# A Mamba layer and six local-attention layers in one kernel: folded value weights, heads on partition quarters, softmax transposed by VectorE

## The chip, the cores and the metric

The kernel runs on one core of one Trainium2 chip. The metric is the time on the device in microseconds (us) of one execution; the median of several is compared. A core has five engines that each follow their own list of instructions in order: TensorE (PE; its weight loads are shown apart as PEld), VectorE (DVE), ScalarE (ACT), GpSimd (POOL) and SyncE (SP), which here issues every DMA. They meet through semaphores alone.

## What is computed

Input x is 4 sequences of 1024 tokens with 128 features. Everything is float32 but the mask.

```python
x = L0_attn_x                                   # (4, 1024, 128)
x = x + mamba_block(layernorm(x))               # two directions, states of 16, 256 channels
x = x + ffn_block(layernorm(x))                 # the six layers below

def ffn_block(x):
    for i in range(6):
        x = attn_layer(shift_tokens(x), Wqkv[i], q_scale[i], k_scale[i], Wo[i]) + x
        x = ffn_layer(shift_tokens(x), ln_g[i], ln_b[i], W1[i], b1[i], W2[i], b2[i]) + x
    return x

def attn_layer(x, Wqkv, qs, ksc, Wo):           # 16 heads of 64
    q, k, v = split_heads(x @ Wqkv)
    q, k = l2norm(q) * qs, l2norm(k) * ksc
    q = q * cos * scale + rotate_half(q) * sin * scale
    k = k * cos / scale + rotate_half(k) * sin / scale
    # windows of 32 queries; the keys are the window before and the window itself, 64 in all
    sim = where(mask, -big, 8.0 * q @ k.T)
    out = softmax(sim) @ v
    return join_heads(out) @ Wo

def ffn_layer(x, g, bln, W1, b1, W2, b2):
    a, gate = split((layernorm(x) * g + bln) @ W1 + b1)
    return a * gelu(gate) @ W2 + b2
```

`shift_tokens` takes half of the features from the token before. The value path of one head is linear in x: softmax times (x @ Wv_h), times Wo_h, summed over heads.

## The kernel before

The work has three stretches. In the first, class `Prepare` runs the Mamba projections, convolutions and gates of eight units (4 sequences, 2 directions) in the order of the table `FIRST_ORDER`, and spills them to DRAM. It also prepares layer data, one layer in each of six units: W1 scaled by the norm's gain, biases, and rotary tables multiplied by the q and k scales (`lf`, `fp`, `fv`, `fa`, `fs`, `lr`, `rm`, `rs`). Class `Beside` runs the Mamba state scan as 512 steps of 128x512: decay (ACT, line 699), input (DVE or POOL, 710 to 714), scan (DVE, 731), output (POOL, 744) and a sum over states on PE (line 766, which writes into partition quarters).

In the second stretch class `Layers` runs the six layers of a sequence that is through while the scan of the following ones goes on; in the third the layers run alone. `Layers` works on 96 tiles (4 sequences, 6 layers, 4 blocks of 256 tokens). For each tile some 130 small operations are named in a table, `ORDER` in the second stretch and `LAST_ORDER` in the third; the number behind the dash says how many tiles back the operation reaches, so about five tiles are under way at a time. The place in the table is the place in every engine's list. Words with x (`xd`, `xi`, `xr`, `xo` and so on) call the scan's steps, six of each a tile.

One tile's attention, with lines: `q` projects 128 tokens onto 512 columns of q or k in eight products (974). `sq` squares them on ACT (981); `rr` and `ro` multiply by the rotary tables on DVE (994); `n` sums the squares (1002); `nr` makes the reciprocal norm on ACT (1014 to 1016); `ra` adds rotated halves on POOL in eight operations (1007); `rs` applies the norm (1020). `t` transposes on PE (1057) and `qk` copies to SBUF (1067). `v` projects the values (1026), `va` copies them (1032) and `vs` issues a DMA that shifts them by 32 partitions (1042, 1043), so that a window's 64 keys stand together. `s` puts the mask into PSUM by a product (1078) and `s` and `z` add the 128 products of 32 queries and 64 keys (1096). `mx` takes the row maxima and `e` subtracts them on DVE (1106, 1112); `ex` takes the exponentials of 128x1024 in one go on ACT (1118); `sm` sums and inverts (1122, 1123), `ew` scales on POOL (1127). `te` transposes the probabilities on PE (1134), `at` copies (1140); `w` and `y` multiply them by the values (1159), `oe` copies (1170) and `pw` multiplies by Wo (1181).

In the feed-forward part `pd` centres the tokens by a product (1207), `fsq` squares, `pvar` averages (1221), `fl` makes the reciprocal deviation, `xnc` and `xn` normalize (1217, 1232). `pg` projects the gate, `ge` adds its bias (1247) and `gelu` follows in two pieces with a table load before and after (1253 to 1256); `pa`, `gm`, `py` and `xs` finish.

PSUM has eight banks; five rotate among all products of `Layers` (`one`), three belong to the scan. Weights of a layer have one buffer each; `weight` counts their uses and, after the last of a layer, queues the loads of the next layer for 30 or 60 table entries later (`later`).

Of the kernel before, what the change touches and what calls it, by code (L numbers as in the profile page):

```python
# [85 lines left out]
def make_masks(nc, pool, c):  # L86
    nc.vector.tensor_copy(c["ident16"], c["ident"])
    nc.vector.memset(c["mean"], 1.0 / D)
    nc.vector.tensor_tensor(c["center"], c["ident"], c["mean"], ALU.subtract)

    m32 = pool.tile([P, 8, 2 * W], F32, name="m32")
    nc.gpsimd.memset(m32, 0.0)
    for r in range(4):
        q = m32[r * W : (r + 1) * W]
        nc.gpsimd.affine_select(
            out=q, in_=q, pattern=[[0, 8], [1, 2 * W]], compare_op=ALU.is_ge,
            fill=NEG, base=0, channel_multiplier=-1,
        )
        nc.gpsimd.affine_select(
            out=q, in_=q, pattern=[[0, 8], [-1, 2 * W]], compare_op=ALU.is_ge,  # L100
            fill=NEG, base=W, channel_multiplier=1,
        )
    nc.vector.tensor_copy(c["mask"], m32)

    nc.vector.tensor_copy(c["mask0"], m32)
    nc.vector.memset(
        c["mask0"][0:W].rearrange("p (h x) j -> p h x j", x=2)[:, :, 0, 0:W], NEG
    )
# [23 lines left out]
class Prepare:  # L132
# [4 lines left out]
    def __init__(self, ctx, tc, c, eps, one, dram, x, lnwb, win, wconv, wx, wdt, rope, qks, tabs,  # L137
                 w1, lvec, w1f, lvf, x1_dram, beside, load):
# [4 lines left out]
        self.folds = w1, lvec, w1f, lvf  # L143
        self.rope = {}
# [204 lines left out]
    def xb(self, u, h):  # L349
        xdbl = u.tile(self.sp, "xdbl", 0, [NX, T], 2)  # L350
        self.nc.vector.tensor_copy(xdbl[:, h * TC : (h + 1) * TC], u.bank["wx", h])
# [50 lines left out]
    def lf(self, u):  # L402
        if u.l is not None:
            w1s = u.tile(self.sp, "w1s", 0, [P, 2 * FI], 2)
# [29 lines left out]

    def fs(self, u):
        if u.l is not None:
            self.nc.sync.dma_start(out=self.folds[2][u.l], in_=u.tiles["w1s", 0])
            self.nc.sync.dma_start(out=self.folds[3][u.l], in_=u.tiles["lv", 0])

# [86 lines left out]
class Beside:  # L526
# [165 lines left out]
    def decay(self):  # L692
        n = self.next("decay", self.limit)
# [28 lines left out]
    def scan(self):  # L722
        n = self.next("scan", self.limit)
# [11 lines left out]
    def output(self):  # L735
        n = self.next("output", self.limit)
# [144 lines left out]
class Layers:  # L881
# [3 lines left out]
    def __init__(  # L885
        self, ctx, tc, c, eps, ps, beside, wqkv, tabs, wo, w1f, w2, lvf, xsa, x1_dram, out
# [3 lines left out]
        self.dram = (wqkv, tabs, wo, w1f, w2, lvf)  # L890
# [12 lines left out]
        self.count = dict.fromkeys(USES, 0)  # L903
# [8 lines left out]
    def weight(self, name, t):  # L912

        w = self.weights[name]
        self.count[name] += 1
        if self.count[name] % (NSB * USES[name]) == 0 and self.tile_at(t, 1):
            for part in self.parts(name, (t.l + 1) % DEPTH):
                self.later(part, LATER if name in ("wos", "w2s") else LATE)
        return w
# [6 lines left out]
    def load(self, name, l):  # L926
        for part in self.parts(name, l):
            part()

    def parts(self, name, l):  # L930

        wqkv, _, wo, w1f, w2, lvf = self.dram
        tile_ = partial(self.wp.tile, dtype=F32, name=name)
        if name in ("w0", "w1", "w2"):
            a = int(name[1]) * H * DH
            w = tile_([P, H * DH])
            pairs = [
                (w[:, i : i + 256], wqkv[l, :, a + i : a + i + 256]) for i in range(0, H * DH, 256)
            ]
        elif name == "wos":  # L940
            w = tile_([P, NHP, D])
            of = wo[l].rearrange("(h p) m -> p h m", p=P)
            pairs = [(w[:, i : i + 2], of[:, i : i + 2]) for i in range(0, NHP, 2)]
# [11 lines left out]
        self.weights[name] = w  # L955
        return [partial(self.nc.sync.dma_start, out=to, in_=of) for to, of in pairs]
# [13 lines left out]
    def q(self, t, i, a, g):  # L970

        w = self.weight(f"w{a}", t)
        pq = t.bank["q", i, a, g] = self.one("pq")
        self.nc.tensor.matmul(  # L974
            pq, lhsT=self.tokens(t, i), rhs=w[:, g * 512 : (g + 1) * 512], start=True, stop=True
        )

    def sq(self, t, i, a, g):
        sq = t.tile(self.sp, "sq", (i, a), [P, H, DH], 2)
        pq = t.bank["q", i, a, g].rearrange("p (h e) -> p h e", e=DH)  # L980
        self.nc.scalar.activation(sq[:, g * 8 : g * 8 + 8], pq, AF.Square)  # L981

    def rr(self, t, i, a, g):

        self.rotary(t, i, a, g, t.tile(self.sp, "r", (i, a), [P, H, DH], 4), 0)

    def ro(self, t, i, a, g):

        self.rotary(t, i, a, g, t.tile(self.sp, "rot", (i, a), [P, H, DH], 2), 1)

    def rotary(self, t, i, a, g, out, x):
        pq = t.bank["q", i, a, g].rearrange("p (h e) -> p h e", e=DH)
        tab = bc(t.tab[:, i, 2 * a + x, :], 1, [P, 8, DH])
        self.nc.vector.tensor_tensor(out[:, g * 8 : g * 8 + 8], pq, tab, ALU.mult)  # L994
        t.rotary += 1
        if t.rotary == 16 and self.tile_at(t, 2):
            self.later(partial(self.table, self.tile_at(t, 2)))

    def n(self, t, i, a):

        n2 = t.tile(self.sp, "n2", i, [P, 2, H], 4)
        self.nc.vector.tensor_reduce(n2[:, a, :], t.tiles["sq", (i, a)], AX.X, ALU.add)  # L1002

    def ra(self, t, i, a, x):
        r, rot = t.tiles["r", (i, a)], t.tiles["rot", (i, a)]
        to, of = slice(x * W, x * W + W), slice(W - x * W, 2 * W - x * W)
        self.nc.gpsimd.tensor_tensor(r[:, :, to], r[:, :, to], rot[:, :, of], ALU.add)  # L1007
# [10 lines left out]
    def rs(self, t, i, a):  # L1018
        r, n2 = t.tiles["r", (i, a)], t.tiles["n2", i]
        self.nc.gpsimd.tensor_tensor(r, r, bc(n2[:, a, :], 2, [P, H, DH]), ALU.mult)  # L1020

    def v(self, t, i, g):

        w = self.weight("w2", t)
        pv = t.bank["v", i, g] = self.one("pv")
        self.nc.tensor.matmul(  # L1026
            pv, lhsT=self.tokens(t, i), rhs=w[:, g * 512 : (g + 1) * 512], start=True, stop=True
        )

    def va(self, t, i, g):  # L1030
        v = t.tile(self.sp, "v", i, [P, H * DH], 4)
        self.nc.scalar.copy(v[:, g * 512 : (g + 1) * 512], t.bank["v", i, g])

    def vs(self, t, i):

        nc, v = self.nc, t.tiles["v", i]
        vs = t.tile(self.sp, "vs", i, [P, H * DH], 4)
        if t.sb == 0 and i == 0:
            nc.gpsimd.memset(vs[0:W], 0.0)
        else:  # L1040
            before = t.tiles["v", 0] if i else self.tile_at(t, -1).tiles["v", 1]
            nc.sync.dma_start(out=vs[0:W], in_=before[P - W : P])
        nc.sync.dma_start(out=vs[W:P], in_=v[0 : P - W])
# [8 lines left out]
    def t(self, t, i, a, g):  # L1052

        rf = t.tiles["r", (i, a)].rearrange("p h e -> p (h e)")
# [16 lines left out]
    def s(self, t, g):  # L1071
# [10 lines left out]
        self.products(t, g, range(2))  # L1082

    def z(self, t, g):
        self.products(t, g, range(2, 4))

    def products(self, t, g, js):
        qT, kT = t.tiles["qT", 0], self.kT
        for j in js:
            for x in range(2):  # L1090
                for r in range(4):
                    at = P * (r // 2) + 64 * x + W * (r % 2)
                    for par in range(2):
                        rows = slice(64 * par, 64 * par + 64)
                        col = (j * 2 + x) * 64
                        self.nc.tensor.matmul(  # L1096
                            t.bank["s", g, par][r * W : (r + 1) * W, col : col + 64],
                            lhsT=qT[rows, g * 4 + j, at : at + W],
                            rhs=kT[rows, g * 4 + j, at : at + 2 * W],
                            start=False, stop=(j == 3 and x == 1),  # L1100
                        )

    def mx(self, t, g, par):
        mx = t.tile(self.sp, "mx", g, [P, 16], 2)
        sv = t.bank["s", g, par].rearrange("p (n j) -> p n j", j=2 * W)
        self.nc.vector.tensor_reduce(mx[:, par * 8 : par * 8 + 8], sv, AX.X, ALU.max)
# [22 lines left out]
    def te(self, t, g, par):  # L1129

        ef = t.tiles["e", g].rearrange("p (h x) j -> p h (x j)", x=2)
        pe = t.bank["te", g, par] = self.one("pe")
        for j in range(4):
            self.nc.tensor.transpose(  # L1134
                pe[:, j * P : (j + 1) * P], ef[:, par * 4 + j, :], self.c["ident"]
            )

    def at(self, t, g, par):
        at = t.tile(self.sp, "at", (g, par), [P, 4, P], 4)
        self.nc.scalar.copy(at, t.bank["te", g, par].rearrange("p (h t) -> p h t", t=P))  # L1140

    def w(self, t, g):

        for x in range(2):
            t.bank["w", g, x] = self.one("po")
        self.weighted(t, g, range(2))

    def y(self, t, g):
        self.weighted(t, g, range(2, 4))

    def weighted(self, t, g, js):
        for j in js:
            for r in range(4):
                v = t.tiles["v" if r % 2 else "vs", r // 2]
                for par in range(2):
                    col = (g * 8 + 2 * j + par) * DH
                    for x in range(2):
                        rows = slice(64 * x, 64 * x + 64)
# [425 lines left out]
```

## Time and profile before

| what | us |
|---|---|
| median of the runs shown (4049.41 to 4068.73) | 4055.16 |
| span of the profiled execution | 4070.2 |
| mean granted TensorE clock | 0.959 of full |

The profiled execution is one run on the chip, 15 us over that median. An engine's busy share is an average over stretches with different limits, so the text that follows reads it by stretch. In a row of a group or of the timeline stand the line, the engine, the operation, the tile written and read, shapes, and behind the x the number of instructions. A float32 product shows as two PE instructions, a transpose as one. In the granted clock, by slices of a fortieth of the span:

```profile
PEclk6788869999999999999999999999999999999999
DMA  5688855555545555555555555554221222122211
```

### The profile page before, as it was taken

How to read it: one execution, taken by the hardware profiler on the slowest of the kernel's cores; microseconds unless marked ns; L12 is line 12 of the kernel's file. 1: busy time of each engine (PE TensorE's matmuls, PEld its weight loads, DVE VectorE, ACT ScalarE, POOL GpSimd, SP SyncE). 2: the span in 40 equal slices, each digit the busy share in tenths (PEclk: the TensorE clock that was granted, in tenths of full speed). 3: DMA queues.
4: the chain of work that ended last, by engine and by line, in shares of the span. 5: the costliest groups of instructions: out<-in, count | busy, mean ns of one | idle time of the engine just before them, and what ended most of it. 6: DMA issues, size and time to landing. Idle time of an engine off the chain costs nothing.

```text
span 4070.2 us, 145466 instructions
## 1 busy us (share of the span) xinstructions
PE 3825.5 (94%) x62248; PEld 2447.0 (60%) x62248; DVE 3397.9 (83%) x5081; ACT 2975.5 (73%) x5581; POOL 3164.3 (78%) x2589
## 2 busy tenths in 40 slices
PE   5899859999999999999999999999999999999998
PEld 1333226666666666666666666666666666666665
DVE  3677769999899999999999999999777777777774
ACT  4577737887777787787777887877667777677775
POOL 2767669999889898998998998988666666566662
PEclk6788869999999999999999999999999999999999
DMA  5688855555545555555555555554221222122211
GB/s 156 190 268 267 250 178 149 148 161 154 149 133 159 145 154 153 161 151 148 154 145 142 156 156 158 153 151 118 58 65 54 64 58 74 52 63 57 66 50 40
DMA packets 319415, 540.05 MB, mean 133 GB/s; under 512 B 41795, under 2 KB 123467, under 8 KB 318771
## 3 DMA queue, kind: packets, MB, share of 16 engines
q1 hardware_dynamic: 318770, 530.75, 45.5%
q8 instruction: 492, 8.06, 0.9%
q14 instruction: 153, 1.25, 0.1%
HBM read 381.42 MB, written 51.67 MB: 106 GB/s over the span
## 4 chain that ended last, share of the span: by engine, by line
PE 70%; ACT 12%; DVE 7%; POOL 6%; issue 4%; DMA 1%; SPq 1%; DVEq 0%; ACTq 0%; POOLq 0%
PE pq L974 12%; PE po L1159 10%; PE pw L1181 8%; PE pv L1026 7%; PE pt L1057 6%; PE sim L1096 5%; PE pe L1134 4%; PE pm L290 3%; PE py L1278 3%; PE pa L1262 3%; PE pg L1238 2%; ACT sq L981 2%; PE acc L766 2%; DVE sh L731 1%; PE sim L1078 1%
## 5 line engine op out<-in xcount | busy, mean ns | idle before, releaser
L1007 POOL TENSOR_TENSOR r<-r,rot 128x512 f32<-128x512 f32 x768 | 964.1, 1274 | 83.2 <-DVE rot L994 71.1
L1020 POOL TENSOR_TENSOR r<-r,n 128x1024 f32<-128x1024 f32 x384 | 726.2, 1905 | 261.3 <-ACT n L1016 253.2
L974 PE MATMUL pq<-w,xsa 128*128 128x512 f32 x1536 | 799.0, 615 | 2.7 <-ACT at L1140 1.6
L744 POOL TENSOR_TENSOR sh<-sh,sc 128x512 f32<-128x512 f32 x512 | 649.9, 1274 | 96.9 <-DVE sh L731 66.7
L981 ACT ACTIVATE sq<-pq 128x512 f32<-128x512 f32 x768 | 448.2, 599 | 254.0 <-PE pq L974 125.4
L994 DVE TENSOR_TENSOR rot<-pq,tab 128x512 f32<-128x512 f32 x768 | 516.4, 683 | 133.9 <-ACT sq L981 111.0
L994 DVE TENSOR_TENSOR r<-pq,tab 128x512 f32<-128x512 f32 x768 | 518.1, 683 | 82.1 <-PE pq L974 40.3
L1127 POOL TENSOR_TENSOR e<-e,sm 128x1024 f32<-128x1024 f32 x192 | 365.5, 1904 | 243.6 <-DVE sm L1123 228.4
L1057 PEld LDWEIGHTS pt<-ident,r 128*128 128x128 f32 x3072 | 359.1, 142 | 242.5 <-issue 119.1
L1057 PE MATMUL pt<-ident,r 128*128 128x128 f32 x3072 | 443.4, 277 | 37.0 <-POOL r L1020 15.2
L1002 DVE TENSOR_REDUCE n<-sq 128x16 f32<-128x1024 f32 x384 | 456.6, 1210 | 0.0
L1159 PEld LDWEIGHTS po<-at,vs 64*64 64x64 f32 x12288 | 332.3, 135 | 198.3 <-issue 153.8
L1159 PE MATMUL po<-at,vs 64*64 64x32 f32 x12288 | 400.0, 223 | 21.5 <-issue 12.3
L1159 PE MATMUL po<-at,v 64*64 64x32 f32 x12288 | 391.6, 220 | 5.9 <-issue 5.8
L1026 PE MATMUL pv<-w,xsa 128*128 128x512 f32 x768 | 383.4, 601 | 0.2 <-ACT qT L1067 0.2
L1181 PE MATMUL pw<-o,wos 128*128 128x256 f32 x1536 | 377.9, 389 | 1.7 <-ACT o L1170 1.7
L731 DVE TENSOR_TENSOR_SCAN sh<-da,carry,sh 128x512 f32<-128x512 f32 x256 | 327.1, 1278 | 43.7 <-ACT da L699 41.2
L731 DVE TENSOR_TENSOR_SCAN sh<-da,sh 128x512 f32<-128x512 f32 x256 | 311.5, 1217 | 57.2 <-ACT da L699 50.6
L1096 PEld LDWEIGHTS sim<-kT,qT 64*32 64x32 f32 x24576 | 264.5, 106 | 141.8 <-issue 134.7
L1159 PEld LDWEIGHTS po<-at,v 64*64 64x64 f32 x12288 | 334.6, 136 | 9.0 <-issue 8.9
L699 ACT ACTIVATE da<-sdt,b_nega 128x512 f32<-128x512 f32 x378 | 260.5, 689 | 108.2 <-DVE sh L731 92.7
L974 PEld LDWEIGHTS pq<-w,xsa 128*128 128x128 f32 x1536 | 257.0, 191 | 125.8 <-issue 49.0
(160 smaller groups left out, 7598.5 us busy)
## 6 DMA issues: line engine op xcount, KB each, us to landing
sdt<-dts SPq DMA_DIRECT2D x756, 256.0 KB
vs<-v SPq DMA_DIRECT2D x192, 384.0 KB
fdt<-dts SPq DMA_DIRECT2D x204, 256.0 KB
w<-in_wqkv SPq DMA_DIRECT2D x288, 128.0 KB
tab<-tabs SPq DMA_DIRECT2D x96, 256.0 KB
vs<-v SPq DMA_DIRECT2D x168, 128.0 KB
wos<-in_wo SPq DMA_DIRECT2D x96, 128.0 KB
dts<-e SPq DMA_DIRECT2D x32, 256.0 KB
```

The costliest lines, as they stand in the source:

```text
L731: self.nc.vector.tensor_tensor_scan(h, self.da.pop(n), h, self.carry[:, at : at + 1] if t else 0.0, ALU.mult, ALU.add)
L744: self.nc.gpsimd.tensor_tensor(h, h, self.unit[k][2], ALU.mult)
L974: self.nc.tensor.matmul(pq, lhsT=self.tokens(t, i), rhs=w[:, g * 512 : (g + 1) * 512], start=True, stop=True)
L981: self.nc.scalar.activation(sq[:, g * 8 : g * 8 + 8], pq, AF.Square)
L994: self.nc.vector.tensor_tensor(out[:, g * 8 : g * 8 + 8], pq, tab, ALU.mult)
L1007: self.nc.gpsimd.tensor_tensor(r[:, :, to], r[:, :, to], rot[:, :, of], ALU.add)
L1020: self.nc.gpsimd.tensor_tensor(r, r, bc(n2[:, a, :], 2, [P, H, DH]), ALU.mult)
L1026: self.nc.tensor.matmul(pv, lhsT=self.tokens(t, i), rhs=w[:, g * 512 : (g + 1) * 512], start=True, stop=True)
L1057: self.nc.tensor.transpose(pt[:, j * P : (j + 1) * P], rf[:, (g * 4 + j) * P : (g * 4 + j + 1) * P], self.c["ident"],)
L1096: self.nc.tensor.matmul(t.bank["s", g, par][r * W : (r + 1) * W, col : col + 64], lhsT=qT[rows, g * 4 + j, at : at + W], rhs=kT[rows, g * ...
L1159: self.nc.tensor.matmul(t.bank["w", g, x][64 * par : 64 * par + 64, j * P + r * W : j * P + (r + 1) * W], lhsT=v[rows, col : col + DH], rh ...
L1181: self.nc.tensor.matmul(t.bank["pw"], lhsT=wos[:, g * 4 + h, :], rhs=t.tiles["o", g][:, h, :], start=(g == 0 and h == 0), stop=(g == 1 and ...
```

## The change

What it does, by part:

- *Values.* The value and output weights of each head are multiplied on chip during the preparation (`wl` loads, `wp` multiplies, `we` copies, `ws` stores; six layers, 16 heads, 128x128 each) and read back by `Layers` as `wvo`. `v` then takes 32 tokens at a time and four products of 512 columns, one for each partition quarter: quarter c has the heads of four columns of `wvo`. `va` copies eight windows a tile. The shifted copies (`vs`) and the output projection (`pw`) go.
- *Scores.* A partition quarter holds one head's 32 queries; a row of a bank has eight windows of 64 keys.
- *Softmax.* `mx` gives the negated maximum; `ea` takes the exponentials window by window from PSUM on ACT, 128x64 each, 32 a tile, with the maximum as bias, and writes out the row sums. `e`, `ex` and the sum in `sm` go; `rc` inverts.
- *Transposing.* `tp` transposes 32x32 blocks of 128x1024 on DVE, twice a tile; `te` and `at` go. `w` multiplies quarters (contraction over four heads and 32 keys at a time, 32 queries by 128 features), `oe` copies once and `ot` transposes the 256x128 result back on PE.
- *Rotary.* q and k columns are stored half by half (on the host), so `ra` is four operations of 128x1024.
- *Feed-forward.* W1 is also centred in the preparation (`fc`, `fe`), so that `xn` takes the uncentred tokens and `xnc` goes. `pg` and `pa` share banks by pairs; Gelu reads PSUM and adds the bias itself.
- *Loads.* Each layer's weights are loaded at a named place in the tables (`lw`, `lwv`, `l`, `ll`, `lt`); values and vectors have two buffers, the others one.
- *Tables.* `FIRST_ORDER`, `ORDER` and `LAST_ORDER` are new throughout; the scan's steps gain guards that skip a call that comes too early.

```diff
+    def wp(self, u, g, par):
+        if u.l is not None:
+            pm = u.bank["wp", g, par] = self.one("pm")
+            rows = slice(64 * par, 64 * par + 64)
+            for k in range(4):
+                self.nc.tensor.matmul(
+                    pm[:, k * D : (k + 1) * D], lhsT=u.tiles["wvl", 0][rows, g * 4 + k, :],
+                    rhs=u.tiles["wol", 0][rows, g * 4 + k, :], start=True, stop=True,
+                )
...
+    def fc(self, u, g):
+        if u.l is not None:
+            pm = u.bank["fc", g] = self.one("pm")[:, 0:FI]
+            self.nc.tensor.matmul(
+                pm, lhsT=self.c["center"], rhs=u.tiles["w1s", 0][:, g * FI : (g + 1) * FI],
+                start=True, stop=True,
+            )
...
-    def ra(self, t, i, a, x):
-        r, rot = t.tiles["r", (i, a)], t.tiles["rot", (i, a)]
-        to, of = slice(x * W, x * W + W), slice(W - x * W, 2 * W - x * W)
-        self.nc.gpsimd.tensor_tensor(r[:, :, to], r[:, :, to], rot[:, :, of], ALU.add)
+    def ra(self, t, i, a):
+        r = t.tiles["r", (i, a)].rearrange("p h x e -> p (h x e)")
+        rot = t.tiles["rot", (i, a)].rearrange("p h x e -> p (h x e)")
+        self.nc.gpsimd.tensor_tensor(r, r, rot, ALU.add)
...
+    def v(self, t, w):
+        wvo = self.weight("wvo", t)
+        pv = t.bank["v", w] = self.one("pv")
+        at = W + t.sb * SB + w * W
+        for c in range(4):
+            self.nc.tensor.matmul(
+                pv[c * W : (c + 1) * W], lhsT=self.xsa[t.b % 2][:, at : at + W], rhs=wvo[:, c],
+                start=True, stop=True,
+            )
...
+    def ea(self, t, g, par):
+        e = t.tile(self.sp, "e", g, [P, 16, 2 * W], 2)
+        sm = t.tile(self.sp, "sm", g, [P, 16], 2)
+        mx = t.tiles["mx", g]
+        sv = t.bank["s", g, par].rearrange("p (n j) -> p n j", j=2 * W)
+        for w in range(8):
+            n = par * 8 + w
+            self.nc.scalar.activation(
+                e[:, n], sv[:, w], AF.Exp, bias=mx[:, n : n + 1], accum_out=sm[:, n : n + 1]
+            )
...
+    def tp(self, t, g):
+        eT = t.tile(self.sp, "eT", g, [P, 2, 8, 2, W], 2)
+        self.nc.vector.transpose(
+            eT.rearrange("p a w x q -> p (a w x q)"),
+            t.tiles["e", g].rearrange("p n j -> p (n j)"),
+        )
+
+    def w(self, t, g, i):
...
+        for par in range(2):
+            for x in range(2):
+                for r in range(4):
...
+                    self.nc.tensor.matmul(
+                        t.bank["o"][r * W : (r + 1) * W, i * D : (i + 1) * D],
+                        lhsT=eT[:, par, 4 * i + r, x, :],
+                        rhs=of.tiles["vw", at % 8][:, 2 * g + par, :],
+                        start=first, stop=(t.weighted == 4 and par == 1 and x == 1),
+                    )
...
     def gelu(self, t):
-        nc.scalar.activation(ge[:, 0:2, :], ge[:, 0:2, :], AF.Gelu)
-        nc.scalar.activation(ge[: FM[2], 2, :], ge[: FM[2], 2, :], AF.Gelu)
+        for m in range(3):
+            k = FM[m]
+            nc.scalar.activation(
+                ge[:k, m, :], self.half(t, "pg", m), AF.Gelu, bias=lv[:k, 3 + m : 4 + m]
+            )
```

## The prediction

> **What bounds the kernel now.** I read the busy table first, then the chain that ended last, then busy time by stretches, to see whether one engine bounds every stage.
>
> ```profile
> PE 3825.5 (94%) x62248; PEld 2447.0 (60%) x62248; DVE 3397.9 (83%) x5081; ACT 2975.5 (73%) x5581; POOL 3164.3 (78%) x2589
> PE 70%; ACT 12%; DVE 7%; POOL 6%; issue 4%; DMA 1%; SPq 1%; DVEq 0%; ACTq 0%; POOLq 0%
> ...
> 800.00:2800.00 2000.00, 1941.36 (x34683) 1298.99 (x34682) 1878.56 (x2733) 1550.25 (x2956) 1822.59 (x1503) 0.99 0.54 151
> 3000.00:4000.00 1000.00, 990.19 (x18409) 687.76 (x18402) 764.86 (x1182) 732.03 (x1403) 639.59 (x455) 1.00 0.21 60
> ```
>
> The last two rows give, for a stretch of the span, busy us (and instructions) of PE, PEld, DVE, ACT and POOL, then the granted clock. PE is busy 97% in the first, where Mamba runs beside the layers, and 99% in the second, where the layers run alone. DVE (94%) and POOL (91%) are close behind in the first. ACT has the most room: 78% and 73%.
>
> Each of the 96 tiles issues the mean-of-squares product (line 1221) once, as two instructions. The first stretch holds 108 of them, so a tile takes 2000/54 = 37.0 us with Mamba; from the start at 3015 to that at 4002 lie 29 tiles, 34.0 us each without. By these starts 63 tiles run beside Mamba and 33 alone; the preparation takes the first 550 us. ACT carries 1550.25/54 = 28.7 us a tile with Mamba and 0.732 x 34.0 = 24.9 without.
>
> **PE.** The timeline gives what a group costs: its start to the start of what follows it.
>
> ```profile
> 3306.22 2.00 PE L1181 MATMUL pw<-o,wos 128*128 128x256 f32 x8
> 3308.14 0.86 PE L1096 MATMUL sim<-kT,qT 64*32 64x64 f32 x64
> ...
> 3312.49 1.04 PE L1134 MATMUL pe<-ident,e 128*128 128x128 f32 x8
> 3313.36 0.41 PE L1057 MATMUL pt<-ident,r 128*128 128x128 f32 x2
> ...
> 946.73 1.07 PE L766 MATMUL acc<-sh,wide 128*32 128x512 f32 x8
> 947.72 0.66 PE L1057 MATMUL pt<-ident,r 128*128 128x128 f32 x4
> ```
>
> Removed a tile: the output projection, 16 instructions, 2 x (3308.14 - 3306.22) = 3.84 us; 16 transposes of the probabilities, 2 x 0.87 = 1.74; the value projection, 8 instructions, whose four from 3302.22 are followed at 3304.04, so 3.64; the weighted sums, 256 instructions, whose 64 from 3329.74 are followed at 3330.80, so 4.24. Together 13.46 us.
>
> Added: line 766 shows what four products into the four partition quarters cost: eight instructions of 512 columns in 0.99 us, so the quarters run at the same time. The new values are eight such fours a tile, 7.9 us; where two stand together the switch (some 0.1 us) goes once, so 7.4. The new weighted sums are 128 instructions of 128 columns on quarters; 12 transposes of 128 columns take 1.31 us (3321.23 to 3322.54), 0.109 each, so 32 groups of four cost 3.5 and with four switches 3.8 us. Two transposes of the result, 0.2. Together 11.4 to 11.9: PE loses about 2.0 us a tile, 1.5 to 2.5. Were the quarters serial, the values alone would cost 32 x 0.87 = 28 us; line 766 excludes that.
>
> The Trainium skill, "TensorE: Matmul & The Clock Gate", section "Why this matters for your kernels", measured three quarter products at 2.38 times, not 3; row 766 is at 3.5 of 4. By the page the values would take 8.7 us and PE would lose only 0.8 us a tile.
>
> **DVE and POOL.** DVE loses four subtractions (line 1112, 0.64 us busy each) and two sums of 1024 (line 1122, 1.21), 5.0 us, and gains two transposes of 128x1024. No row shows one: from 0.68 (half the elements, line 1112) to 2.42 (twice line 1122). I take 1.21, the row of that size. DVE goes from 1878.56/54 = 34.8 to 32.2 us, at worst 34.6. POOL's rotary sums go from eight of 1.27 to four of 1.91 (line 1020) to 2.35 (line 245): 0.8 to 2.5 us less of 33.8. Neither binds; PE covers both. The copies of values to shifted partitions (line 1043) go, 95 MB and most of SP's waits, but PE waits 0.6 us in all for them: worth nothing.
>
> **ACT, where it is decided.** Gone: the long exponentials (201.8/96 = 2.10 us a tile), the copies after the transposes (218.3: 2.27), four result copies (206.2: 2.15), the normalized copy (0.37), and the bias pass and Gelus (238.5: 2.48): 9.4 us. Added: four more value copies (2.33), one 256-wide copy (0.37), three Gelus with a bias from PSUM (1.45 as line 1247): 4.2. So -5.2 us. Then 32 exponentials of 64 columns a tile, each with a bias from a tile and a sum written out; the whole program has 3072. Nearest rows:
>
> ```profile
> 3315.46 0.32 ACT L1016 ACTIVATE n<-n,t_lift 128x32 f32<-128x32 f32 x1
> 3315.69 0.56 ACT L1067 COPY qT<-pt 128x512 f32<-128x512 f32 x1
> ...
> L853 ACT ACTIVATE rstd_s<-rstd_s 128x4 f32<-128x4 f32 x8 | 1.6, 206 | 0.3
> ```
>
> A 128x32 one with a bias holds ACT for 0.23 us before the next starts, though it lasts 0.32: ends overlap by 0.09. 32 more elements add (1.05 - 0.60)/512 x 32 = 0.03. No row writes a sum out. Below: it is free, 0.23 to 0.26 each. Above: the sum is an instruction of its own of the shortest kind (0.206) and nothing overlaps, 0.35 + 0.21 = 0.56. I take a short instruction that overlaps like others, 0.26 + 0.11 = 0.37, nearest to the rows that run back to back: 11.7 us a tile. ACT then has 28.7 - 5.2 + 11.7 = 35.2 us with Mamba and 31.4 alone, against PE's 35.0 and 32.0 (its waits of before included).
>
> The Trainium skill, "VectorE: DVE Perf Modes", section "Two Vector instructions with no wait between them", says that an operation which writes out its accumulator is two instructions. It speaks of VectorE, and no run here shows ScalarE. It speaks against this change; by it the free end falls away.
>
> So the spare engine becomes a second full one. ACT now idles some 8 us of each tile in waits on PE and DVE, and the new tables must hide nearly all of it. Each lost margin shows twice: behind a burst of eight exponentials (3.0 us) wait the copies that empty PE's banks, and five banks serve them all. I allow 1.1 us over ACT with Mamba, 36.3 (-0.7), and 0.9 over PE alone, 32.9 (-1.1); the allowance is my estimate, from the 1.1 us that PE idles a tile (3%) where it is the bound now.
>
> **Preparation.** Six units each gain two 512 KB loads, 1 MB of stores, 16 folding products (32 instructions, 3.5 us) and two centring ones (4 of 341 columns, 1.1 us), and ACT six copies (2.6 us). PE's clock there is 0.73 to 0.82, so 4.6/0.8 = 5.8 us a unit, 35 in all since PE is busy 90% in these iterations. Bounds: 0, hidden in waits; 50, where the 12.6 MB at 250 GB/s add to a DMA share of 0.87 between 200 and 400 us. The moved weight loads land one layer's data in single buffers; 256 KB lands in 4 to 7 us by the chain, and the shortest distance in the tables, from lw01 to its product, is 29 of 176 entries, 6 us: at most 1 us for each of 23 layer changes, 0 to 23, taken as 0.
>
> **Sum.** 63 x -0.7 = -44; 33 x -1.1 = -36; +35: -45 on the profiled 4070.2 us. The median of the runs shown is 4055.2, 15 lower, so 4010.
>
> **Rivals.**
> 1. *The sum comes almost free, 0.25 each.* ACT 31.5 and 27.7; PE stays the bound at 35.2 and 32.1: -113 - 63 + 35 = -141, 3914. For: overlaps in every ACT row. Against: a result more has to leave the engine. With 0.23 and preparation hidden, 3870.
> 2. *ACT is the bound (slower).* Place: the 32 exponentials. At 0.46, midway to the upper bound, ACT has 38.2 and 34.4, with 1.2 over it periods of 39.4 and 35.6: +151 + 53 + 35 = +239, 4294. At 0.56: 41.4 and 37.6, periods 42.6 and 38.8, +353 + 158 + 35 = +546, 4601. It decides from about 0.39, where ACT's excess takes back what PE gives. For: the chosen price is 0.02 below that point.
> 3. *No change.* Gains in the layers equal the preparation: exponentials at 0.37 to 0.39, 4035 to 4075.
> 4. *The quarters serialize*, from 1.2 us for a four (PE then gains): for: another tile size between groups; against: row 766. At 1.5 us, +4 x 96 = 384, 4440.
>
> **How the numbers follow.** Chances: my forecast 0.36, the free sum 0.17, ACT as the bound 0.33, no change 0.12, serial quarters 0.02. A measurement of this kernel tells about 0.5% (20 us) from none. Faster takes the forecast and the free sum, less a little for the forecast's edge at 4035: 0.52; same 0.12; slower 0.36. Range 3890 to 4300: below is the free sum, above ACT at 0.46; the serial quarters, the upper third of rival 2 and the last of rival 1 stay out. The forecast's own range is 3960 to 4035.
>
> **What would show it.** In the profile after: rows of 128x64 exponentials start to start (0.37), and whether an instruction stands between them; eight value instructions in 0.9 to 1.0 us; PE's removed rows gone; tile periods 36.3 and 32.9 by the line of the mean of squares; the preparation 35 us longer; DVE's transpose at 1.2. Wrong would be: ACT under 90% busy with PE idle (banks or order, not load), or exponentials dearer than 0.39.

## The result and the profile after

The changed kernel takes 4270.26 us (median of four executions, 4263.56 to 4271.7) against 4053.76 of the kernel before beside it: ratio 1.0518, 95% interval 1.0492 to 1.0544. It is slower by 5.2%; 4010 was forecast, 1.1% faster. The profiled execution has a span of 4269.9 us. From its page, the busy table and the shares of the chain that ended last (followed back from the last instruction, at each step to what released it):

```profile
PE 3721.9 (87%) x52479; PEld 1990.6 (47%) x52480; DVE 3139.8 (74%) x4697; ACT 3417.6 (80%) x10993; POOL 3092.5 (72%) x2181
...
ACT 33%; DVE 28%; PE 22%; POOL 7%; issue 5%; DMA 3%; SPq 0%; ACTq 0%; DVEq 0%; POOLq 0%
```

PE held 70% of the chain before and holds 22% now, but no engine took its place: the chain goes to and fro between ACT and DVE. By stretches, in the columns used for the kernel before:

```profile
800.00:2800.00 2000.00, 1757.01 (x26896) 948.79 (x26892) 1611.17 (x2327) 1656.42 (x5531) 1658.67 (x1186) 0.99 0.37 114
3200.00:4200.00 1000.00, 933.37 (x15400) 552.62 (x15399) 685.68 (x1077) 872.19 (x3095) 620.81 (x335) 1.00 0.10 30
```

Beside Mamba PE is busy 88%, and DVE, ACT and POOL 81 to 83%: four engines, none full. By the starts of the mean of squares (line 1273 here) a tile takes 39.98 us beside Mamba (36.93 before, by the same count over tiles 3 to 60) and 33.61 alone (34.05), and the first comes at 689.9 us instead of 650.6. So the preparation is 39 us longer. From the first tile's start to the 64th's, beside Mamba, the time grows by 189 us; from there to the last tile's start, alone, it falls by 26; the tail behind that is 3 shorter. That is the 199.7 us between the two spans.

The prices of the new instructions, from the timeline:

```profile
3524.60 2.78 PE L1089 MATMUL pv<-wvo,xsa 128*32 128x512 f32 x24
3527.31 1.98 PE L1035 MATMUL pq<-qk,xsa 128*128 128x512 f32 x4
...
3518.30 0.31 ACT L1168 ACTIVATE e<-sim,mx 128x64 f32<-128x64 f32 x1
3518.52 0.19 ACT L1168 ACTIVATION_READ_ACCUMULATOR e<-sim,mx 128x1 f32 x1
3518.61 0.30 ACT L1168 ACTIVATE e<-sim,mx 128x64 f32<-128x64 f32 x1
...
3509.08 1.24 DVE L1200 STREAM_TRANSPOSE eT<-e 128x1024 f32<-128x1024 f32 x1
```

Three fours of values take 2.71 us, 0.90 each. An exponential with its sum is two instructions, yet the next starts 0.3 us later (0.289 in the middle of a burst). The transpose takes 1.24. These are near the prediction's prices or under them, so the loss needs another cause.

The timeline of one place in a tile, ACT first and then DVE:

```profile
1537.35 0.60 ACT L1042 ACTIVATE sq<-pq 128x512 f32<-128x512 f32 x1 [1.63 <-DVE r L1055]
1537.97 1.28 ACT L1308 ACT_TABLE_LOAD   x1
1539.26 1.19 ACT L1308 ACTIVATE ge<-pg,lv 128x256 f32<-128x256 f32 x3
1540.47 1.28 ACT L1312 ACT_TABLE_LOAD   x1
1541.77 0.60 ACT L1042 ACTIVATE sq<-pq 128x512 f32<-128x512 f32 x1
...
1537.34 1.16 DVE L1060 TENSOR_REDUCE n<-sq 128x16 f32<-128x1024 f32 x1
1542.39 0.69 DVE L1055 TENSOR_TENSOR rot<-pq,tab 128x512 f32<-128x512 f32 x1 [3.90 <-ACT sq L1042]
```

In brackets stand the idle time ahead of an instruction and what ended it. The table says `gelu-4 sq011-1 ro011-1`: the order of the words also fixes who reads the bank first. ACT does the Gelu with two table loads, 3.8 us, and only then the square of the fourth half of q; DVE's rotary product reads the same bank and waits 3.90 us until that square ends. The waits between the squares and the rotary products over the 2000 us from 800, engine, what it waited for, us in all, times and longest:

```profile
DVE rot L1055 <- ACT sq L1042: 197.1, 89, 4.2
ACT sq L1042 <- DVE r L1055: 183.8, 136, 1.7
DVE r L1055 <- ACT sq L1042: 143.1, 139, 2.5
```

524 us, 10.5 in each of 50 tiles. The same rows of the kernel before:

```profile
ACT sq L981 <- DVE r L994: 73.8, 103, 1.7
DVE r L994 <- ACT sq L981: 11.8, 10, 1.3
ACT sq L981 <- DVE rot L994: 9.3, 10, 1.5
DVE rot L994 <- ACT sq L981: 1.5, 4, 0.4
```

Together 96 us, 1.8 a tile.

### The profile page after: what moved, and what is told of

Its sections match the earlier page's. It is cut to its first block, busy times and chain, and to the rows that moved or that the text cites. A ratio compares the mean times of both kernels' runs of the same rounds, so it can differ in the third digit from the quotient of the medians.

```text
span 4269.9 us, 128994 instructions
## 1 busy us (share of the span) xinstructions
PE 3721.9 (87%) x52479; PEld 1990.6 (47%) x52480; DVE 3139.8 (74%) x4697; ACT 3417.6 (80%) x10993; POOL 3092.5 (72%) x2181
## 4 chain that ended last, share of the span: by engine, by line
ACT 33%; DVE 28%; PE 22%; POOL 7%; issue 5%; DMA 3%; SPq 0%; ACTq 0%; DVEq 0%; POOLq 0%
ACT e L1168 10%; DVE r L1055 8%; ACT sq L1042 7%; DVE rot L1055 7%; DVE sh L780 4%; PE pv L1089 4%; PE po L1222 3%; POOL r L1081 3%; PE pq L1035 3%; ACT L1308 3%; ACT ge L1308 3%; ACT da L746 2%; PE pm L289 2%; POOL r L1067 2%; DVE n L1060 2%
## 5 line engine op out<-in xcount | busy, mean ns | idle before, releaser
L1067 POOL TENSOR_TENSOR r<-r,rot 128x1024 f32<-128x1024 f32 x384 | 909.8, 2369 | 343.1 <-DVE sm L1174 199.0
L1168 ACT ACTIVATE e<-sim,mx 128x64 f32<-128x64 f32 x3072 | 920.8, 355 | 33.0 <-DVE mx L1156 30.8
L1089 PE MATMUL pv<-wvo,xsa 128*32 128x512 f32 x6144 | 766.5, 605 | 182.2 <-ACT kT L1120 92.9
L1035 PE MATMUL pq<-qk,xsa 128*128 128x512 f32 x1536 | 805.8, 624 | 80.4 <-DVE rot L1055 66.8
L1168 ACT ACTIVATION_READ_ACCUMULATOR e<-sim,mx 128x1 f32 x3072 | 749.4, 249 | 0.0
L1096 ACT COPY vw<-pv 128x512 f32<-128x512 f32 x768 | 434.4, 625 | 23.7 <-PE pv L1089 22.4
L1089 PEld LDWEIGHTS pv<-wvo,xsa 128*32 128x32 f32 x6144 | 154.6, 109 | 603.2 <-issue 214.9
L1222 PE MATMUL po<-vw,eT 128*32 128x128 f32 x12096 | 382.0, 274 | 34.1 <-issue 28.8
L1035 PEld LDWEIGHTS pq<-qk,xsa 128*128 128x128 f32 x1536 | 255.9, 194 | 317.1 <-DVE rot L1055 85.1
L1222 PEld LDWEIGHTS po<-vw,eT 128*32 128x32 f32 x12096 | 331.8, 110 | 75.4 <-issue 41.0
```

The source lines that it names most:

```text
L1035: self.nc.tensor.matmul(pq, lhsT=self.tokens(t, i), rhs=w, start=True, stop=True)
L1067: self.nc.gpsimd.tensor_tensor(r, r, rot, ALU.add)
L1089: self.nc.tensor.matmul(pv[c * W : (c + 1) * W], lhsT=self.xsa[t.b % 2][:, at : at + W], rhs=wvo[:, c], start=True, stop=True,)
L1168: self.nc.scalar.activation(e[:, n], sv[:, w], AF.Exp, bias=mx[:, n : n + 1], accum_out=sm[:, n : n + 1])
L1222: self.nc.tensor.matmul(t.bank["o"][r * W : (r + 1) * W, i * D : (i + 1) * D], lhsT=eT[:, par, 4 * i + r, x, :], rhs=of.tiles["vw", at % 8 ...
```

## The experiments

Two theories: "load" (the 32 exponentials make ACT a second full engine) and "order" (the new tables make ACT and DVE wait for each other over the q banks). The ratios are to runs of the kernel before taken beside each kernel; their medians go from 4053.76 to 4068.47 us, so a difference between two medians of this table can be off by some 15 us, and the ratios and tile times are the better guide.

| kernel | us | ratio to before, interval | tile beside Mamba | tile alone |
|---|---|---|---|---|
| as changed | 4270.26 | 1.0518 (1.0492 to 1.0544) | 39.98 | 33.61 |
| Gelu one place later | 4152.08 | 1.0208 (1.0186 to 1.0229) | 37.92 | 33.55 |
| rotary products first | 4147.79 | 1.0202 (1.0183 to 1.0220) | 37.81 | 33.62 |
| one exponential a bank | 4182.93 | 1.0294 (1.0264 to 1.0325) | 39.25 | 32.26 |
| no folding products | 4243.90 | 1.0439 (1.0412 to 1.0466) | 40.07 | 33.52 |
| one square later, alone | 4250.65 | 1.0455 (1.0439 to 1.0472) | 39.97 | 32.71 |
| table beside reordered | 3999.89 | 0.9844 (0.9818 to 0.9870) | 35.49 | 33.58 |
| both tables reordered | 3962.93 | 0.9758 (0.9735 to 0.9781) | 35.38 | 32.49 |
| both, one exponential | 3929.62 | 0.9671 (0.9639 to 0.9703) | 35.37 | 31.68 |
| before, short exponentials | 4896.80 | 1.2039 (1.2008 to 1.2070) | 45.21 | 43.27 |
| before, both reordered | 4077.39 | 1.0022 (1.0012 to 1.0032) | 37.21 | 34.02 |

**Gelu one place later.**

```diff
-qk011-2 xt-0 qk101-2 rc1-3 q011-1 sq010-1 v1-3 xq-0 v4-3 n00-1 xa-0 gelu-4 sq011-1 ro011-1 v0-3
+qk011-2 xt-0 qk101-2 rc1-3 q011-1 sq010-1 v1-3 xq-0 v4-3 n00-1 xa-0 sq011-1 gelu-4 ro011-1 v0-3
```

> One word of the table beside Mamba changes place with its neighbour: the Gelu (with its two table loads, 3.8 us on ACT) is issued behind the square of q's fourth half instead of ahead of it. No instruction is added or taken away. Theory 'order' (ACT and DVE read the same q banks in turn, and the new table puts long ACT work between two squares that DVE waits for): DVE's wait of 3.9 us at this place in each tile goes, the tile beside Mamba gets 1 to 2.5 us shorter, 63 tiles, so 4110 to 4210 us. Theory 'load' (32 exponentials fill ACT, wherever they stand): ACT has the same work, 4250 to 4290 us.

The one swap gives 118 us, more than half of the loss: 2.06 us on each tile beside Mamba, next to nothing alone. In the same 2000 us:

```profile
DVE rot L1055 <- ACT sq L1042: 10.5, 46, 0.6
DVE r L1055 <- ACT sq L1042: 238.7, 145, 3.2
```

DVE's waits of `rot` for squares fall from 197.1 to 10.5 us, those of `r` rise from 143.1 to 238.7; with ACT's waits for `r` the three rows fall from 524 to 382.

**Rotary products first.** The swap also moved the square ahead on ACT. This run issues the two rotary products ahead of the Gelu and the square instead. Between their old place and the new one stands no other word for DVE, so no engine's list changes: in the two traces PE, DVE, ACT and POOL run the same groups of instructions in the same order. What changes is who waits for whom at the bank.

```diff
-... n00-1 xa-0 gelu-4 sq011-1 ro011-1 v0-3
-q110-1 rr011-1 xa-0 ...
+... n00-1 xa-0 ro011-1 rr011-1 gelu-4 sq011-1 v0-3
+q110-1 xa-0 ...
```

> The changed kernel; in the table beside Mamba DVE's two rotary products of q's fourth half are issued ahead of the Gelu, so that they read their bank before the square does. On ACT nothing changes place: Gelu and its table loads still stand ahead of that square. Theory 'bank in turn' (the square and the two products never read the bank at one time, and who is issued second waits for the first): DVE's wait of 3.9 us goes just as with the swap of Gelu and square, 4120 to 4190 us. Theory 'ACT's order' (the swap helped because the square, the sum of squares behind it or the value copies came earlier on ACT): ACT has the old order, 4250 to 4280 us.

The same gain: 122 us, 2.17 a tile beside Mamba. Its timeline at the same place:

```profile
1534.89 1.28 ACT L1308 ACT_TABLE_LOAD   x1
1536.19 1.19 ACT L1308 ACTIVATE ge<-pg,lv 128x256 f32<-128x256 f32 x3
1537.40 1.28 ACT L1312 ACT_TABLE_LOAD   x1
1538.69 0.60 ACT L1042 ACTIVATE sq<-pq 128x512 f32<-128x512 f32 x1
...
1535.34 0.68 DVE L1055 TENSOR_TENSOR rot<-pq,tab 128x512 f32<-128x512 f32 x1
1535.93 0.68 DVE L1055 TENSOR_TENSOR r<-pq,tab 128x512 f32<-128x512 f32 x1
```

DVE reads its bank while the Gelu runs, and the square comes as late as ever without harm. So it is the turn at the bank that cost, not the place of the Gelu on ACT.

**One exponential a bank.**

```diff
-        for w in range(8):
-            n = par * 8 + w
-            self.nc.scalar.activation(
-                e[:, n], sv[:, w], AF.Exp, bias=mx[:, n : n + 1], accum_out=sm[:, n : n + 1]
-            )
+        n = par * 8
+        self.nc.scalar.activation(
+            e[:, n : n + 8], sv, AF.Exp, bias=mx[:, n : n + 1], accum_out=mx[:, n + 1 : n + 2]
+        )
...
```

> The eight exponentials of a bank become one of 512 columns with one maximum and one sum for eight windows (left out: the maxima and sums of the other seven windows, so the softmax is not normalized per window); the reciprocal reads two sums and writes sixteen. ACT does 28 exponentials and 28 sum reads less in each tile: 9.25 us become about 2.5, -6.7. Theory 'load': the tile beside Mamba falls from 40.0 to about 36 us and below 33 alone, 63 x -4 and 33 x -1, so about 3990 us (3940 to 4060). Theory 'order': the squares still stand behind the Gelu and its table loads, the tile beside Mamba loses less than 2 us: 4130 to 4270 us.

```profile
800.00:2800.00 2000.00, 1765.76 (x27423) 970.60 (x27422) 1642.66 (x2373) 1377.83 (x2786) 1692.87 (x1212) 0.99 0.40 117
```

ACT falls from 33.1 to 27.0 us busy a tile beside Mamba, yet the tile loses 0.73 us; alone it loses 1.35. In all 87 us for a fifth of ACT's work: load is not what held the stretch beside Mamba.

**No folding products.**

```diff
     def fc(self, u, g):
-        if u.l is not None:
+        if False:
...
     def wp(self, u, g, par):
-        if u.l is not None:
+        if False:
```

(`fe` and `we` likewise.)

> In the preparation the folding products (16 for the values, 2 for the centring, in each of six units) and the copies that empty their banks are left out, while the loads and stores of the weights stay; the layers then run on weights that are not folded. Theory 'PE and ACT': the 39 us that the preparation got longer are those products, the first mean of squares comes at about 655 us and the time is 25 to 40 us shorter, 4230 to 4245. Theory 'transfers': the 12.6 MB do it, less than 12 us shorter, 4258 to 4272.

26 us shorter by the medians (32 by the ratios); the first mean of squares comes at 657.3 us instead of 689.9. The products and their copies are 33 of the preparation's 39 us, loads and stores at most 7.

**Short exponentials in the kernel before.**

```diff
...
-            e[:, s], sv, bc(t.tiles["mx", g][:, s], 2, [P, 8, 2 * W]), ALU.subtract
+        for w in range(8):
+            n = par * 8 + w
+            self.nc.scalar.activation(
+                e[:, n], sv[:, w], AF.Exp, bias=mx[:, n : n + 1], accum_out=sm[:, n : n + 1]
+            )
...
-... mx01-2 e00-2 e01-2 ... ex0-2 ... sm0-2
+... mx01-2 ea00-2 ea01-2 ... rc0-2
```

> One part of the change alone in the kernel before: the 32 short exponentials with bias and sum take the place of DVE's four subtractions, the two long exponentials and DVE's two sums (ACT +7.1 us a tile at 0.289 each, DVE -5.0), at the places of the old table where subtraction and sum stood; the matrix products stay as they were. Theory 'load': ACT at 28.7 + 7.1 = 35.8 of 37.0 us beside Mamba becomes a second full engine and the tile grows by 2 to 3 us, alone by 1: 4180 to 4280 us. Theory 'order': the exponentials cost only where they stand ahead of a square or of a copy that empties a bank, and the table of before has 8 us of waits of ACT to put them in: within 1 us a tile, 4000 to 4140 us.

Both theories missed: 4896.8. ACT's work came out as priced (950.32 us busy in 1200, 35.8 a tile), but the tile grew to 45.2, so ACT idles too. Two bursts a tile, each of 16 exponentials in 4.85 us, stand where subtractions on DVE stood, and PE waits behind them. The windows, in the columns above, and two waits from PE's timeline:

```profile
1200.00:2400.00 1200.00, 1056.56 (x16897) 692.22 (x16898) 804.10 (x1183) 950.32 (x3073) 889.40 (x721) 0.92 0.44 124
...
1490.00:1495.00 5.00, 4.71 (x148) 2.78 (x138) 4.48 (x6) 4.94 (x13) 4.92 (x6) 1.00 0.84 242
1495.00:1500.00 5.00, 1.41 (x46) 1.30 (x46) 0.09 (x1) 5.00 (x29) 1.56 (x2) 0.89 0.17 54
1500.00:1505.00 5.00, 5.00 (x101) 4.22 (x98) 3.03 (x6) 2.03 (x5) 1.90 (x1) 0.50 0.35 108
1505.00:1510.00 5.00, 5.00 (x135) 3.07 (x135) 3.75 (x6) 3.88 (x10) 2.72 (x3) 0.93 0.18 63
```

```profile
1496.52 0.30 PE L1157 MATMUL po<-at,vs 64*64 64x32 f32 x2 [1.81 <-ACT e L1115]
1498.89 0.33 PE L1157 MATMUL po<-at,vs 64*64 64x32 f32 x3 [2.07 <-ACT e L1115]
```

After the two waits PE has a granted clock of 0.50, by these windows for about 6.8 us. How the 8.3 us that the tile grew divide between the waits and this clock was not tried apart. As an estimate from the mean clock, 0.92 here against 0.99 before, the clock can take at most 0.08 x 45.2 - 0.01 x 36.9 = 3.2 of them. As for the tables: the old order with this softmax is far worse than the new tables, so the change needed new ones.

**One square later, alone.**

```diff
-... ra00-1 sq000-1 z0-2 sq010-1 rc1-3 ro010-1
+... ra00-1 z0-2 sq010-1 rc1-3 sq000-1 ro010-1
```

> The changed kernel; in the table for the layers alone one word moves: the square of q's first half goes behind the square of its third half and the reciprocal, four places later. Theory 'order': the circle of 33.4 us has DVE's products and ACT's squares in turn in it (12.5% and 10% rotary products, 6.7% squares of a tile's chain), and one hand-over less takes 0.5 to 1.2 us off a tile, 33 tiles: 4230 to 4255 us. Theory 'load': nothing, 4262 to 4275.

0.90 us less on each tile alone, 20 us in all, as "order" had it: here too the order costs time that the engines' work does not ask for.

**The tables reordered.** First the table beside Mamba (27 of 176 words moved), then `LAST_ORDER` too (12 of 141). The core of the first:

```diff
-qk011-2 xt-0 qk101-2 rc1-3 q011-1 sq010-1 v1-3 xq-0 v4-3 n00-1 xa-0 gelu-4 sq011-1 ro011-1 v0-3
-q110-1 rr011-1 xa-0 va0-3 va1-3 xo-0 xr-0 va4-3 t110-2 xy-0 n01-1 qk110-2 xd-0 rr110-1 sq110-1
-q111-1 sq111-1 rr111-1 ra01-1 xo-0 ro110-1 ...
+xt-0 qk101-2 rc1-3 q011-1 sq010-1 v1-3 rr010-1 v4-3 xa-0 gelu-4 ro011-1 v0-3 q110-1 rr011-1 sq011-1
+xa-0 n00-1 xo-0 va0-3 va1-3 xi-0 xr-0 t110-2 xq-0 sq110-1 xy-0 qk110-2 xd-0 n01-1 rr110-1 va4-3
+q111-1 rr111-1 s0-2 sq111-1 xo-0 ro110-1 ra01-1 ...
```

> Only the order of the words in the table beside Mamba differs from the changed kernel (some thirty of 176 words moved by a few places, mostly squares and q products ahead of Gelu, value copies and exponentials; Mamba's own words hold their number): every engine has the same instructions. Theory 'order': DVE's wait for squares (6.8 us a tile) and ACT's for rotary products (3.7) mostly go, and the tile beside Mamba comes down from 40.0 to between PE's own 35.1 us of busy time and 37: 63 x (-3.0 to -4.9), so 3960 to 4080 us. Theory 'load' (ACT's 33 us of work and bursts of exponentials need about 4 us of margin in any order): no better than the swap of one word, 4130 to 4180.

> As before, and the table for the layers alone is reordered too (the reciprocal and the weighting of the first half of the heads, the squares and the rotary products moved by a few places). Theory 'order': the regular 33.4 us of a tile alone is a circle of hand-overs (sums, weighting, transpose, rotary products, squares, maxima, exponentials) and not PE's work (186 of 200 us busy, 31.1 us a tile); it comes down by 0.7 to 1.8 us, 33 tiles: 25 to 60 us under the run with the table beside Mamba alone. Theory 'load': PE's work is 32.0 by the prediction and ACT's 28.9, so within 15 us of that run.

Both came as "order" had it: 270 us from the first table, 37 more from the second, and with both the kernel is 2.4% faster than before. In the windows of this kernel PE binds again, and the largest wait between squares and rotary products beside Mamba is one row of 41.2 us (45.5 in all, 0.8 a tile):

```profile
800.00:2800.00 2000.00, 1927.49 (x30345) 1087.39 (x30345) 1833.74 (x2629) 1858.87 (x6229) 1866.06 (x1324) 1.00 0.43 128
3000.00:3800.00 800.00, 778.88 (x12868) 454.10 (x12869) 576.41 (x889) 721.79 (x2568) 517.58 (x278) 1.00 0.11 33
```

```profile
DVE r L1055 <- ACT sq L1042: 41.2, 93, 1.4
```

PE is busy 96 and 97%, with ACT, DVE and POOL at 92 to 93% beside Mamba. What each of the moved words is worth, beyond the one tried alone in each table, was not tried.

**Both tables and one exponential.** The two edits together.

> Both reordered tables, and the eight exponentials of a bank as one (left out: the maxima and sums of seven of eight windows, as in the earlier run with one exponential), ACT -6.7 us a tile. In the kernel as changed this gave 87 us. Theory 'load': once the order is mended ACT is the next bound, so 2 us or more a tile: 150 us or more under the run with both tables. Theory 'order': PE is the bound by then and ACT's work is hidden, under 1 us a tile: 0 to 80 us under it.

33 us: alone 0.81 x 33 = 27, beside Mamba 0.01 us a tile. With the order mended, ACT's load costs nothing beside Mamba and under 1 us alone.

**The control.** Both tables of the kernel before, reordered in the same manner (17 of 179 and 7 of 140 words moved by a few places).

> The control: the kernel before with both of its tables reordered in the same way, none of the change in it. PE idles 1.1 us of 37.0 a tile beside Mamba and 0.4 of 34.0 alone, so no order can give more than about 63 x 1.1 + 33 x 0.4 = 82 us: 3975 to 4055. If the change itself earns what the mended order showed, this stays above the run with both tables reordered (3963 us); if the gain there was the reordering alone, it comes to 3963 or below.

No gain, 4077.39 against 4068.47. That is one order and not a search; but by the 82 us that PE idles (an estimate) no order of the kernel before gets under 0.980 of its time, and both tables reordered stand at 0.9758 (0.9735 to 0.9781). So at least a part of the gain is the change's own, and by this control all of it, once its order doesn't take it back.

## Why the prediction was wrong

- **The step that failed** is the allowance: "I allow 1.1 us over ACT with Mamba, 36.3 (-0.7), and 0.9 over PE alone, 32.9 (-1.1)", taken from PE's idle time in a kernel where PE was full. Measured beside Mamba: 40.0 us, 4.9 over PE's 35.1 and 6.9 over ACT's 33.1. What stood there was the order: in it squares and rotary products wait for each other 10.5 us a tile, and with the same instructions in the mended order the tile takes 35.5. The text said that "the new tables must hide nearly all of it" and never looked whether they do, though the new table, with `gelu-4` ahead of a square, was there to be read, and the trace of the kernel before already had squares waiting for rotary products (73.8 us in the same 2000).
- **The sum.** Between the two profiled spans the change costs 199.7 us where -45 was forecast, 245 off. Of these 233 are beside Mamba (-44 forecast, +189 measured), 11 alone (-36 forecast, -26 measured), 4 in the preparation, less 3 in the tail. The rest of the 260 us between 4010 and 4270 is the 15 us that the forecast took off because the profiled execution of before lay over its median; that of the changed kernel lies at its median.
- **The rivals.** "ACT is the bound" gave 4294, near the time, but by the wrong mechanism, so that is luck: ACT is 83% busy and its exponentials cost 0.289. "Almost free" had the price of the exponentials nearer (0.25), but not the second instruction, and its lower end of 3870 does not come out of its terms (-113 - 63 without the preparation gives 3879). The quarters did not serialize (0.90 a four). What happened was named only under "Wrong would be: ACT under 90% busy with PE idle (banks or order, not load)", with no price and no chance. The time lies inside the stated 3890 to 4300 by the same luck; the forecast was faster and the kernel is slower.
- **PE.** The prices held: values 8.0 us a tile against 7.4 to 7.9 (8.7 was the estimate by the page cited there), 0.90 for a four against 0.99. The forecast of 35.0 held 1.1 us of waits, so 33.9 of work; PE is busy 35.1 a tile in the changed kernel and 34.1 with both tables reordered. Then the tile falls by 1.55 us beside Mamba and 1.56 alone, the low end of the forecast's 1.5 to 2.5. Its own terms, 13.46 less 11.4 to 11.9, give 1.6 to 2.1, so "about 2.0" was at their favourable end.
- **DVE and POOL.** DVE is busy 32.2 us a tile as forecast, the transpose took 1.24 for 1.21, POOL's long sums 2.37 for 2.35.
- **ACT** was mis-sized: an exponential costs 0.289 for 0.37, so ACT is busy 33.1 us for 35.2. The split into two instructions was right. The Trainium skill's page "VectorE: DVE Perf Modes", section "Two Vector instructions with no wait between them", states for VectorE that an operation which writes out its accumulator is two instructions; the rows show the same on ScalarE.
- **Preparation.** 39 us more for 35, 33 of them the products and their copies, as worked out.
- **Transfers** were taken at nothing: 540 MB became 454, and no run tries them apart.

## What to carry to other kernels

When a kernel is hand-ordered and a change frees the full engine, forecast the order too: look in the new order for long work (a table load, a burst) ahead of an instruction that hands a bank to another engine, and price that wait from the trace of before. Two readers of one PSUM bank were a chain here; whichever reader has long work ahead of it in its list should read second. With every engine under 90% busy, as here, look for an order to mend, and mend it before the change is judged.

## What the hardware showed

- Squares on ACT and rotary products on DVE that read the same bank never overlapped: of 736 pairs (the first 46 tiles) in each of four kernels none does, and the nearest are 0.03 us apart. The second always waits for the first. So with not one instruction moved in any engine's list, a different turn at the bank was worth 122 us of 4270. The Trainium skill, "PSUM — Partial Sum Buffer", section "PSUM bank collisions raise a hardware error", says that two engines, two readers too, must be kept apart by bank and quarter. In these traces they are kept apart; no run here lets them meet, so what would happen then is not shown.
- An exponential of 128x64 with its sum takes ACT 0.289 us from start to start: about 0.2 to the sum's own instruction and 0.09 from there to the next.
- In the kernel before with short exponentials a wait cost twice. After waits of 1.81 and 2.07 us, with two products between them, the granted clock was 0.50 for about 6.8 us, and 64 products that take 1.06 us took 1.86. The Trainium skill, "TensorE: Matmul & The Clock Gate", section "HAM oscillation — how this bites in real kernels", describes such a gate and gives as its rule no idle gap of TensorE over some 3.4 us. Here each wait is shorter and only the two together, 3.88 us, are longer, so two short waits that stand close can do it. In the changed kernel the clock stays at 0.99 beside Mamba, as before, so it has no part in its loss.
